# Selective scan of a four-layer network: VectorE's product goes to PSUM in one buffer, most decays go to SBUF and run three tiles ahead

## The chip, the cores and the metric

The kernel runs on one core of a Trainium2 chip as one program. The metric is device time in microseconds (us) from the first to the last instruction, the median of three runs. The core has five instruction queues that run side by side and meet through semaphores: TensorE (PE, with its weight loads shown as PEld), VectorE (DVE), ScalarE (ACT), GpSimd (POOL) and SyncE (SP, whose queue SPq issues the transfers). Each queue is worked off in its order, so an instruction that waits holds up all that stands behind it.

## The reference: what is computed

Four layers follow one another on a batch of 8 images of 56 x 56 pixels and 128 channels. Layers 0, 2 and 3 are deformable convolutions with their norms and feed-forward parts. Layer 1 is a visual state-space block, and the change is in it alone. It normalises and projects the image to 256 channels, convolves it, and then runs four scans over the pixels (rows and columns, forward and backward), each with 16 states for a channel:

```python
xs = jnp.stack([x0, x1, x0[..., ::-1], x1[..., ::-1]], axis=1)
...
dt = jax.nn.softplus(dt + dt_projs_b[None, :, :, None])
A = -jnp.exp(A_logs).reshape(K, Di, N)

def step(h, t):
    dt_t, u_t, B_t, C_t = t
    h = h * jnp.exp(dt_t[..., None] * A) + (dt_t * u_t)[..., None] * B_t[:, :, None, :]
    y = jnp.einsum('bkdn,bkn->bkd', h, C_t)
    return (h, y)
```

`exp(dt*A)` is called the decay here, `(dt*u)*B` the input of the scan. The four results are summed, normalised, gated, projected and put through a feed-forward part.

## The kernel before

The layers run one after the other: `tile_net` builds a `Dcn` for layers 0, 2 and 3 and a `Vss` for layer 1. The change is in `Vss.scans`, in its pools in `Vss.run`, and in one argument of the program's constructor.

**Tiling.** A step is one image, one of four directions `k`, and one of four chunks `c` of 784 pixels: 8 x 4 x 4 = 128 steps. Within a step there are 32 tiles of 128 partitions x 784 elements in fp32. A tile holds 32 channels x 4 states: `cg` counts 8 groups of channels, `sg` 4 groups of states, and `order` runs `sg` fastest. That makes 4096 tiles, listed in `units`. Four tiles with one `cg` are called a group below: 1024 groups.

**What a tile needs.** `decay` (L1343) makes `dA = exp(dt*A)` on ScalarE. `inputs` (L1348) makes the input: for `sg` 0 to 2 it is `u` on VectorE, from `dtu` (in PSUM) and `b` (in SBUF); for `sg` 3 it is `up` on GpSimd, from SBUF alone. The scan (L1449) is one VectorE instruction, which takes the decay, the input and a start value `st`, and writes `h` into SBUF. ScalarE saves the last column in `st` (L1452). GpSimd multiplies `h` by `c` (L1454) into `hc`. `add_sums` (L1372) lets TensorE add the products of two tiles into `acc`; `open_sums` (L1364) begins such a sum and `close_sums` (L1380) copies it out through ScalarE. `spread` (L1335) makes `dtu` for a whole group: two matmuls against the identity copy `dt*x` into PSUM.

**Buffers.** PSUM has room for eight banks of 512 elements. `misc` and `acc` take one each, `dtu` one buffer of two banks, and `dA` two buffers of two banks. In SBUF `u` has two buffers, `up` one, `h` three, `hc` six, and `dt` three.

**Order.** The loop over `units` (L1405) writes the instructions down in this order for the tile `now`: due sums, a piece of the next step's preparation, fetches, the decay of tile `now + 1`, the input of tile `now + 1` if it is VectorE's, at `sg == 1` the `spread` for the next group, the input two tiles ahead if it is GpSimd's, and then the scan of tile `now`. At its end `advance` adds a piece of background work: the first stage of the next image, or the last stage of this one, whose statistics run on VectorE and whose matmuls share the bank `misc`. A scheduler then moves instructions within that order. In the built program a group without background work stands on VectorE as u0 u1 s0 s1 u2 s2 s3, where s is a scan and the digit is `sg`.

`add_sums` is tied behind the last `spread` on TensorE by `issue_after`.

Of the kernel before, what the change touches and what calls it, by code (L numbers as in the profile page):

```python
# [41 lines left out]
F32 = mybir.dt.float32  # L42
BF16 = mybir.dt.bfloat16
I32 = mybir.dt.int32
AF = mybir.ActivationFunctionType
ALU = mybir.AluOpType
AX = mybir.AxisListType
PSUM = bass.MemoryType.PSUM
# [70 lines left out]
SC, SR = 784, 14  # L119
# [14 lines left out]
NCG, NSG = DI // TC, NST // TS  # L134
# [342 lines left out]
class Dcn:  # L477
# [9 lines left out]
    def run(self):  # L487
        tc, nc = self.tc, self.nc
        with ExitStack() as ctx:
            enter = ctx.enter_context  # L490
            self.cp = enter(tc.tile_pool(name="c_const", bufs=1))
            self.img = enter(tc.tile_pool(name="c_img", bufs=1))
            self.fp = enter(tc.tile_pool(name="c_front", bufs=1))
            self.up = enter(tc.tile_pool(name="c_unit", bufs=1))
            self.bp = enter(tc.tile_pool(name="c_block", bufs=3))
            self.tp = enter(tc.tile_pool(name="c_tail", bufs=1))
            self.pt = enter(tc.tile_pool(name="c_pt", bufs=3, space=PSUM))
            self.py = enter(tc.tile_pool(name="c_py", bufs=2, space=PSUM))
            self.pm = enter(tc.tile_pool(name="c_pm", bufs=3, space=PSUM))
            self.w = self.net.dcn_weights(self.layer, self.const)  # L500
            self.constants()
            self.split_bias()
            self.loop()
            self.check()
        over = nc.values_load(self.net.flag[:1, :1], min_val=0, max_val=1, skip_runtime_bounds_check_because="a comparison's result")
        with tc.If(over > 0):
            self.net.dcn_slow(self.layer, self.images, self.src, self.dst)
# [479 lines left out]
        nc.vector.tensor_scalar(net.flag, most, 0.0, None, ALU.is_gt)  # L987


class Vss:  # L990


# [6 lines left out]
    def run(self):  # L999
        tc = self.tc  # L1000
        with ExitStack() as ctx:
            enter = ctx.enter_context
            self.cp = enter(tc.tile_pool(name="v_const", bufs=1))
            self.img = enter(tc.tile_pool(name="v_img", bufs=1))
            self.prep = enter(tc.tile_pool(name="v_prep", bufs=1))
            self.work = enter(tc.tile_pool(name="v_work", bufs=2))
            self.bg = enter(tc.tile_pool(name="v_bg", bufs=1))
            self.dram = enter(tc.tile_pool(name="v_dram", bufs=2, space=DRAM))
            self.pmisc = enter(tc.tile_pool(name="v_misc", bufs=1, space=PSUM))
            self.pdtu = enter(tc.tile_pool(name="v_pdtu", bufs=1, space=PSUM))  # L1010
            self.pda = enter(tc.tile_pool(name="v_pda", bufs=2, space=PSUM))
            self.pacc = enter(tc.tile_pool(name="v_pacc", bufs=1, space=PSUM))
            self.weights()
            self.scans()
# [285 lines left out]
    def scans(self):  # L1300
        nc, w = self.nc, self.w
# [6 lines left out]
        units = [(at, t) for at in range(len(steps)) for t in range(NT)]  # L1308
# [13 lines left out]
        def advance(count):  # L1322
            for _ in range(count):
                while tasks:
                    try:
                        next(tasks[0])
                        break
                    except StopIteration:
                        tasks.popleft()

        def on_pool(t):

            return order[t][1] == NSG - 1

        def spread(at, t):  # L1335

            s, (cg, sg) = state[at], order[t]
            ps = s["dtu", cg] = self.pdtu.tile([128, 2, 512], F32, name="dtu", tag="dtu")
            for b in range(2):
                last = nc.tensor.matmul(ps[:, b, :SH], lhsT=self.net.ident, rhs=s["dt", cg][:, 1, SH * b : SH * (b + 1)], start=True, stop=True)  # L1340
            self.last_spread = last.ins

        def decay(at, t):  # L1343
            (i, k, c), s, (cg, sg) = steps[at], state[at], order[t]
            da = s["dA", t] = self.pda.tile([128, 1024], F32, name="dA", tag="dA")
            nc.scalar.activation(da[:, :SC], s["dt", cg][:, 0], AF.Exp, scale=w["A"][:, k, NSG * cg + sg : NSG * cg + sg + 1])  # L1346

        def inputs(at, t):  # L1348
            s, (cg, sg) = state[at], order[t]
            if on_pool(t):  # L1350
                u = self.work.tile([128, SC], F32, name="up", tag="up", bufs=1)
                nc.gpsimd.tensor_mul(u, s["dt", cg][:, 1], s["b", sg])  # L1352
            else:
                u = self.work.tile([128, SC], F32, name="u", tag="u", bufs=2)
                halves = [v.rearrange("p (x e) -> p x e", x=2) for v in (u, s["b", sg])]
                nc.vector.tensor_mul(halves[0], s["dtu", cg][:, :, :SH], halves[1])  # L1356
            s["u", t] = u
# [39 lines left out]
                    tasks.extend(self.output_stage(i, e) for e in (2 * c + 1, 2 * c))  # L1397

        spread(*units[0])
        decay(*units[0])  # L1400
        inputs(*units[0])
        st = ready = None
        group, late = [], deque()
        zeros = self.zeros()
        for now, (at, t) in enumerate(units):  # L1405
            (i, k, c), s, (cg, sg) = steps[at], state[at], order[t]
            forward = k < 2
            if t == 0:
                if at % NSC == 0:
                    st = self.prep.tile([128, NT], F32, name="st", tag="st", bufs=2)  # L1410
                    nc.gpsimd.memset(st, 0.0)
                if at % (NDIR * NSC) == 0 and i + 1 < self.images:
                    tasks.append(self.input_stage(i + 1))
                ready = iter(())
                if at + 1 < len(steps):
                    if steps[at + 1][0] > i:
                        self.load_xb(i + 1)
                    ready = self.prepare(state[at + 1], *steps[at + 1][1:])
            if t % (2 * NSG) == 0:
                late.append((now + 5, open_sums, (at, t)))  # L1420
            while late and late[0][0] <= now:
                _, do, args = late.popleft()
                do(*args)
            if t % 2 == 0:
                next(ready, None)

            if sg == 1:
                to = divmod(NCG * at + cg + 2, NCG)
                if to[0] < len(steps):
                    self.fetch_dt(state[to[0]], to[1])  # L1430
            if t in (3, 19):
                next(zeros, None)

            for x, when in enumerate(((25, 28, 29, 30), (26, 29, 30, 31))):
                if t in when and at + 1 < len(steps):
                    self.fetch_row(state[at + 1], x, when.index(t))
            if now + 1 < len(units):
                decay(*units[now + 1])
                if not on_pool(units[now + 1][1]):
                    inputs(*units[now + 1])  # L1440

                if sg == NSG - 3 and now + 3 < len(units):
                    spread(*units[now + 3])
            if now + 2 < len(units) and on_pool(units[now + 2][1]):
                inputs(*units[now + 2])
            hh = self.work.tile([128, SC], F32, name="h", tag="h", bufs=3)
            step = 1 if forward else -1
            u, dA = s.pop(("u", t)), s.pop(("dA", t))
            nc.vector.tensor_tensor_scan(hh[:, ::step], dA[:, :SC][:, ::step], u[:, ::step], st[:, t : t + 1], ALU.mult, ALU.add)  # L1449
            if c != (NSC - 1 if forward else 0):  # L1450
                last = SC - 1 if forward else 0
                nc.scalar.copy(st[:, t : t + 1], hh[:, last : last + 1])  # L1452
            hc = self.work.tile([128, SC], F32, name="hc", tag="hc", bufs=6)
            nc.gpsimd.tensor_mul(hc, hh, s["c", sg])  # L1454
            group.append((order[t], hc))
            if t % 2:
                late.append((now + 3, add_sums, (at, group)))
                group = []
                if t % (2 * NSG) == 2 * NSG - 1:
                    late.append((now + 5, close_sums, (at, t)))  # L1460
            if t % 2 or t % 4 == 0 or (i == self.images - 1 and k == 2):
                advance(1)
# [81 lines left out]
```

## Time and profile before

| what | value |
|---|---|
| time, median of 3 runs | 18469.42 us (18464.81 to 18477.36) |
| span of the profiled execution | 18479.8 us |
| layer 0, up to the first scans | 0 to 2366 us |
| scans of layer 1 | 2366 to 13801 us: 11435 us |
| layers 2 and 3 | 13801 to 18480 us: 4679 us |
| VectorE busy in the scans | 10264.5 us of 11435 |
| GpSimd busy in the scans | 10454.6 us of 11435 |
| ScalarE busy in the scans | 7051.7 us of 11435 |
| TensorE busy in the scans | 8638.3 us of 11435 |
| one VectorE scan, from `u` | 1838 ns, 3072 times |
| one VectorE `u` | 957 ns, 3072 times |
| one GpSimd `hc`, one `up` | 1873 ns, 4096 times; 1856 ns, 1024 times |
| one ScalarE decay | 915 ns, 4096 times |

The profiled execution is 10.4 us longer than the median of the runs. A duration in the profile reaches to the acknowledged end of an instruction; the next instruction of the same engine can start before that, so the distance from start to start can be shorter than the duration. Idle time of an engine is listed with what ended it (its releaser). In a row of the timeline, "x2" means that two equal instructions were merged.

### The profile page before, as it was taken

The page shows a single profiled execution, that of the slowest core. Times are in us where ns is not written, and L with a number is a line of the kernel's source. Part 1 is how long each engine was busy: PE and PEld are TensorE (multiplying, and loading weights), DVE is VectorE, ACT ScalarE, POOL GpSimd, SP SyncE. Part 2 cuts the span into 40 slices and gives each one's busy share as a digit, 9 for nine tenths or more (in the row PEclk, how much of TensorE's full clock was granted, in tenths as well). Part 3 has the DMA queues.
Part 4 walks back from the last instruction along what each step waited for, and adds up shares of the span by engine and source line. Part 5 has one row for each costly group of instructions (what it writes and reads, how often), then busy time and mean ns, then how long its engine had stood idle before and what let it go on. Part 6 is the DMA issues. An engine that isn't in the chain of part 4 may idle for free. (4 is left out here: it accounts for less than half of the span.)

```text
span 18479.8 us, 257190 instructions
## 1 busy us (share of the span) xinstructions
PE 13780.6 (75%) x89795; PEld 6844.2 (37%) x89795; DVE 15510.8 (84%) x18797; ACT 11145.4 (60%) x20690; POOL 11801.5 (64%) x6462
## 2 busy tenths in 40 slices
PE   5777787678678778678778768767665888577777
PEld 4555422222222222222222222222224666455555
DVE  8888379988988988988988898898985887688886
ACT  4666565566566566566566656656554666456666
POOL 2221089998998998998998998899981111222221
PEclk7878888889889889889888888888886888677777
DMA  7777444444443444344343443443433777577777
GB/s 215 205 210 200 122 158 160 162 158 148 142 149 137 146 147 140 140 150 139 140 150 136 143 152 135 143 150 136 147 122 110 196 198 198 143 204 204 201 204 175
DMA packets 1341779, 2961.90 MB, mean 160 GB/s; under 512 B 91168, under 2 KB 892132, under 8 KB 1325836
## 3 DMA queue, kind: packets, MB, share of 16 engines
q1 hardware_dynamic: 1340460, 2945.21, 51.4%
q8 instruction: 718, 11.76, 0.3%
q14 instruction: 601, 4.92, 0.1%
HBM read 2243.88 MB, written 866.92 MB: 168 GB/s over the span
## 5 line engine op out<-in xcount | busy, mean ns | idle before, releaser
L1454 POOL TENSOR_TENSOR hc<-h,c 128x784 f32<-128x784 f32 x4096 | 7560.9, 1873 | 764.2 <-DVE h L1449 534.4
L1449 DVE TENSOR_TENSOR_SCAN h<-dA,st,u 128x784 f32<-128x784 f32 x3072 | 5569.9, 1838 | 316.2 <-ACT dA L1346 182.3
L1346 ACT ACTIVATE dA<-dt,v_A 128x784 f32<-128x784 f32 x4096 | 3742.8, 915 | 719.1 <-DVE h L1449 717.8
L1356 DVE TENSOR_TENSOR u<-dtu,b 128x784 f32<-128x784 f32 x3072 | 2875.7, 957 | 559.9 <-PE dtu L1340 555.5
L1378 PE MATMUL acc<-hc,v_sum 128*32 128x392 f32 x16384 | 3222.3, 552 | 105.8 <-POOL hc L1454 105.6
L1340 PE MATMUL dtu<-dt,ident 128*128 128x392 f32 x4096 | 2105.1, 642 | 1512.1 <-issue 1102.6
L736 POOL TENSOR_TENSOR ay<-hat,om 112x756 f32<-112x756 f32 (+2 forms) x192 | 525.8, 2738 | 2750.0 <-ACT hat L727 2346.6
L1449 DVE TENSOR_TENSOR_SCAN h<-dA,st,up 128x784 f32<-128x784 f32 x1024 | 1876.7, 1833 | 242.4 <-POOL hc L1454 176.7
L1352 POOL TENSOR_TENSOR up<-dt,b 128x784 f32<-128x784 f32 x1024 | 1900.3, 1856 | 132.1 <-DVE h L1449 110.8
L807 ACT COPY st<-pt 128x448 f32<-128x448 f32 (+1 forms) x2240 | 1177.8, 542 | 1216.4 <-PE pt L805 1210.1
L1452 ACT COPY st<-h 128x1 f32<-128x1 f32 x3072 | 581.7, 189 | 2159.0 <-DVE h L1449 2150.5
L1340 PEld LDWEIGHTS dtu<-dt,ident 128*128 128x128 f32 x4096 | 862.0, 235 | 2564.6 <-issue 1672.2
L775 DVE TENSOR_TENSOR win<-win,patch 112x252 f32 (+2 forms) x3456 | 1695.4, 503 | 124.4 <-DVE win L775 34.2
L805 PE MATMUL pt<-ident,sw 112*128 112x112 f32 (+2 forms) x8960 | 1609.7, 310 | 199.1 <-DMA sw<-skew 198.8
L1378 PEld LDWEIGHTS acc<-hc,v_sum 128*32 128x32 f32 x16384 | 769.8, 117 | 2488.2 <-issue 1675.4
L766 POOL MEMSET win<- 128x1820 f32 (+2 forms) x384 | 630.1, 1646 | 1466.2 <-DMA skew<-win 1159.6
L821 PE MATMUL yps<-st,xw 128*32 128x48 f32 (+5 forms) x35840 | 1077.7, 245 | 397.6 <-ACT st L807 394.8
L805 PEld LDWEIGHTS pt<-ident,sw 112*128 112x128 f32 (+2 forms) x8960 | 1119.5, 161 | 485.6 <-DMA sw<-skew 166.9
L772 DVE TENSOR_TENSOR patch<-ay,hat 112x756 f32<-112x756 f32 (+2 forms) x1152 | 1221.3, 1066 | 22.5 <-POOL ay L736 19.5
L821 PEld LDWEIGHTS yps<-st,xw 128*32 128x32 f32 (+2 forms) x35840 | 757.0, 126 | 825.9 <-ACT st L807 476.1
L1112 PE MATMUL misc<-xn,v_tap 128*128 128x448 f32 x2016 | 867.3, 574 | 96.5 <-ACT xn L1146 61.2
L725 ACT ACTIVATE hat<-om,taps 112x252 f32<-112x252 f32 x1280 | 755.7, 729 | 287.1 <-DVE patch L772 273.4
(165 smaller groups left out, 19517.2 us busy)
## 6 DMA issues: line engine op xcount, KB each, us to landing
dt<-dds SPq DMA_DIRECT2D x1024, 784.0 KB
b<-rows SPq DMA_DIRECT2D x512, 392.0 KB
c<-rows SPq DMA_DIRECT2D x512, 392.0 KB
dds<-dd SPq DMA_DIRECT2D x256, 784.0 KB
sw<-skew SPq DMA_DIRECT2D x224, 812.0 KB
sw<-skew SPq DMA_DIRECT2D x224, 672.0 KB
sw<-skew SPq DMA_DIRECT2D x224, 588.0 KB
xw<-table SPq DMA_DIRECT2D x224, 320.0 KB
```

The lines of the kernel that those rows point to most:

```text
L772: nc.vector.tensor_mul(patch[:n], bcast(a, 3, KX), bcast(b, 2, KY))
L775: self.last_add = nc.vector.tensor_add(to, to, patch[:n, NCB * p : NCB * (p + 1)]).ins
L805: last = nc.tensor.transpose(ps[:m, n * g : n * (g + 1)], sw[:n, g, p : p + m], self.net.ident[:n, :n])
L807: nc.scalar.copy(st[:m], ps[:m, : G * n])
L821: self.nc.tensor.matmul(yps[CG * g : CG * (g + 1), t0:t1], lhsT=xw[:m, k + part, CG * g : CG * (g + 1)], rhs=st[:m, at + t0 : at + t1], st ...
L1340: last = nc.tensor.matmul(ps[:, b, :SH], lhsT=self.net.ident, rhs=s["dt", cg][:, 1, SH * b : SH * (b + 1)], start=True, stop=True)
L1346: nc.scalar.activation(da[:, :SC], s["dt", cg][:, 0], AF.Exp, scale=w["A"][:, k, NSG * cg + sg : NSG * cg + sg + 1])
L1352: nc.gpsimd.tensor_mul(u, s["dt", cg][:, 1], s["b", sg])
L1356: nc.vector.tensor_mul(halves[0], s["dtu", cg][:, :, :SH], halves[1])
L1378: nc.tensor.matmul(acc[r : r + TC, :SH], lhsT=w["sum"], rhs=hc[:, SH * b : SH * (b + 1)], start=False, stop=sg == NSG - 1)
L1449: nc.vector.tensor_tensor_scan(hh[:, ::step], dA[:, :SC][:, ::step], u[:, ::step], st[:, t : t + 1], ALU.mult, ALU.add)
L1454: nc.gpsimd.tensor_mul(hc, hh, s["c", sg])
```

## The change

Five edits, all but the last in `Vss`:

- VectorE's `u` is put into PSUM, in a pool `v_pu` of one buffer of two banks; before, it was in SBUF with two buffers.
- The decays of the tiles with `sg` 0 to 2 go to SBUF, with four buffers. The decay of `sg` 3 stays in PSUM under the name `dAp`, and its pool has one buffer in place of two. PSUM is as full as before: 1 + 1 + 2 + 2 + 2 banks.
- Decays are written down three tiles ahead (`AHEAD`), before it was one.
- VectorE's input is written down with its own tile, just ahead of the scan that reads it; before, it was one tile ahead. `spread` for the next group follows at `sg == 2` and no longer at `sg == 1`. GpSimd's input stays two tiles ahead.
- The scratch space for descriptors of DMAs made by software is set to 8192 bytes a partition, half of the default.

```diff
+AHEAD = 3
...
-            self.pda = enter(tc.tile_pool(name="v_pda", bufs=2, space=PSUM))
+            self.pda = enter(tc.tile_pool(name="v_pda", bufs=1, space=PSUM))
+            self.pu = enter(tc.tile_pool(name="v_pu", bufs=1, space=PSUM))
...
-            da = s["dA", t] = self.pda.tile([128, 1024], F32, name="dA", tag="dA")
-            nc.scalar.activation(da[:, :SC], s["dt", cg][:, 0], AF.Exp, scale=w["A"][:, k, NSG * cg + sg : NSG * cg + sg + 1])
+            if on_pool(t):
+                da = s["dA", t] = self.pda.tile([128, 1024], F32, name="dAp", tag="dAp")[:, :SC]
+            else:
+                da = s["dA", t] = self.work.tile([128, SC], F32, name="dA", tag="dA", bufs=4)
+            nc.scalar.activation(da, s["dt", cg][:, 0], AF.Exp, scale=w["A"][:, k, NSG * cg + sg : NSG * cg + sg + 1])
...
-                u = self.work.tile([128, SC], F32, name="u", tag="u", bufs=2)
+                u = self.pu.tile([128, 1024], F32, name="u", tag="u")[:, :SC]
...
-        decay(*units[0])
-        inputs(*units[0])
+        for x in range(AHEAD):
+            decay(*units[x])
...
-            if now + 1 < len(units):
-                decay(*units[now + 1])
-                if not on_pool(units[now + 1][1]):
-                    inputs(*units[now + 1])
-
-                if sg == NSG - 3 and now + 3 < len(units):
-                    spread(*units[now + 3])
+            if now + AHEAD < len(units):
+                decay(*units[now + AHEAD])
+            if not on_pool(t):
+                inputs(at, t)
+            if sg == NSG - 2 and now + 2 < len(units):
+                spread(*units[now + 2])
...
-            nc.vector.tensor_tensor_scan(hh[:, ::step], dA[:, :SC][:, ::step], u[:, ::step], st[:, t : t + 1], ALU.mult, ALU.add)
+            nc.vector.tensor_tensor_scan(hh[:, ::step], dA[:, ::step], u[:, ::step], st[:, t : t + 1], ALU.mult, ALU.add)
...
-    nc = bacc.Bacc("TRN2", target_bir_lowering=False, num_devices=1)
+    nc = bacc.Bacc("TRN2", target_bir_lowering=False, num_devices=1, dynamic_dma_scratch_size=8192)
```

In the built program a group without background work now stands on VectorE as u0 s0 u1 s1 u2 s2 s3.

## The prediction

> **What bounds the kernel now.** I read the windows by stage first, then what VectorE waited for inside the scans, then VectorE's timeline, instruction by instruction. The windows give us, then the busy time of each engine with its instruction count:
>
> ```profile
> core 0: us, PE busy (x) PEld busy (x) DVE busy (x) ACT busy (x) POOL busy (x), PEclk, DMA share, GB/s
> ...
> 2366.00:13801.00 11435.00, 8638.25 (x31302) 3030.31 (x31302) 10264.50 (x8600) 7051.73 (x13027) 10454.60 (x5762) 0.86 0.41 145
> ```
>
> VectorE is busy for 90% of the scans and GpSimd for 91%: two engines near full that feed each other. ScalarE, at 62%, is not a limit by its sum. What VectorE waited for in that window (us in total, times, longest):
>
> ```profile
> DVE u L1356 <- PE dtu L1340: 473.5, 258, 7.8
> DVE h L1449 <- ACT dA L1346: 234.3, 199, 4.2
> DVE h L1449 <- POOL hc L1454: 214.4, 165, 3.2
> ```
>
> So late decays cost VectorE 234 us, a full set of `h` buffers 214 us, and a late `dtu` 474 us. VectorE's timeline (start, us, instruction) shows what it pays to wait for itself:
>
> ```profile
> 2504.72 0.95 DVE L1356 TENSOR_TENSOR u<-dtu,b 128x784 f32<-128x784 f32 x1
> 2505.58 1.84 DVE L1449 TENSOR_TENSOR_SCAN h<-dA,st,up 128x784 f32<-128x784 f32 x1
> 2507.34 0.95 DVE L1356 TENSOR_TENSOR u<-dtu,b 128x784 f32<-128x784 f32 x1
> 2508.21 1.84 DVE L1449 TENSOR_TENSOR_SCAN h<-dA,st,u 128x784 f32<-128x784 f32 x1
> 2510.08 0.97 DVE L1356 TENSOR_TENSOR u<-dtu,b 128x784 f32<-128x784 f32 x1
> ...
> 8009.96 0.95 DVE L1356 TENSOR_TENSOR u<-dtu,b 128x784 f32<-128x784 f32 x1
> 8011.04 1.85 DVE L1449 TENSOR_TENSOR_SCAN h<-dA,st,u 128x784 f32<-128x784 f32 x1
> 8012.81 1.82 DVE L1449 TENSOR_TENSOR_SCAN h<-dA,st,up 128x784 f32<-128x784 f32 x1
> ```
>
> The scan at 2508.21 reads the `u` of 2504.72. It starts 0.87 us after the `u` in front of it, before that one's 0.95 us are over: neighbours that don't depend on each other overlap. The `u` at 2510.08 goes into the buffer that the scan just before it read (every second `u` has the same one): it starts 1.87 us after that scan, where 2505.58 to 2507.34 took 1.76. The scan at 8011.04 reads the `u` directly before it: 1.08 us from start to start. I took these distances over all starts in the window:
>
> - `u` then a scan that doesn't read it: median 0.881 us (1250 pairs); a scan that reads it: 1.083 us (610 pairs). A wait for a write just made costs 0.202 us.
> - scan then a `u` into another buffer: 1.742 us; into the buffer just read: 1.874 us (108 pairs). That wait costs 0.132 us.
>
> A clean group before is thus 0.865 + 0.882 + 1.757 + 1.742 + 1.083 + 1.767 + 1.742 = 9.84 us. Of the 1023 distances from one group's last scan to the next's, 315 lie between 9.5 and 10 us and the 25th percentile is 9.84: in a third of its groups VectorE's own instructions set the pace. The mean is 11.17.
>
> **The change part by part.**
>
> *One buffer for u, written just ahead of its scan.* In the built order every scan of `u` waits for VectorE itself, and every second and third `u` of a group waits for the scan before it. Neighbours of the first kind rise from 610 to 2509 (elsewhere a statistic of the background work stands between and fills the wait), of the second kind from 108 to 1703:
> 1899 x 0.202 = +384 us, 1595 x 0.132 = +211 us, together +595 us. A clean group becomes 3 x 1.083 + 2 x 1.874 + 1.767 + 1.742 = 10.51 us, +0.67. All of it lies on VectorE, behind which stand the scan, then GpSimd's `hc` and ScalarE's `st`. What could hide it is a wait at the same scan for another engine; those are the 234 and 214 us, which I count as removed below, not twice.
>
> The Trainium skill speaks against this price, on VectorE: DVE Perf Modes, section "The DRAIN you can't avoid": chained copies cost the same with a semaphore after each as with one at the end. By that rule these 595 us would be nothing and the sum would be a gain of 325 us. This trace disagrees, 1.083 against 0.881 us, and I go by the trace.
>
> *u in PSUM instead of SBUF.* No VectorE row before writes PSUM, so the acknowledgement that the scan waits for has no price. From below: ScalarE's decay (to PSUM) overlaps its successor by some 0.062 us where its copies to SBUF overlap by 0.101, so a write to PSUM may end 0.04 us sooner: 2509 x -0.04 = -100 us. From above: the tail of `u` (0.951 less 0.865) doubled, 2509 x 0.086 = +216 us. I take 0, as `u` already reads PSUM and keeps its form.
>
> Another rule of the skill would add to it: Perfetto Trace Analysis, section "Optimizing Scalar/DVE Operations", puts VectorE's fixed access at about 60 ns for SBUF and 125 ns for PSUM. By it the 3072 writes would cost some 200 us more (an estimate from that page); no row here shows it.
>
> *The scan reads dA from SBUF and u from PSUM.* One operand in each, as before. The two kinds of scan differ by 5 ns in the mean (1838 and 1833): 0, within 3072 x 0.015 = 46 us either way by their medians (1841 and 1826).
>
> *Decays three tiles ahead, in five buffers.* Three more of them may be in flight than VectorE needs next, some 8 us of cover, while ScalarE's longest background piece (two table loads of 1.28 us around an operation of 1.51) is 4.1 us. I take nine tenths of the 234 us away: -210 us; bounds 0 and -234. A decay into SBUF costs ScalarE no more: its SBUF operation L1268 of the same size has 855 ns against 915. Decays are moved past `st` copies (L1452), which wait for scans; they no longer wait themselves for a scan one tile back (718 us of ScalarE's idle time). They issue no transfer. The transfer of `dt` waits for the last decay on the old buffer (4123 us of SPq's waits): that one and the next use both come two tiles earlier. 0.
>
> *GpSimd.* Its starts are 1.805 us apart at best: 5120 x 1.805 + 508 of the preparation's (968 us) + 106 for L1189 + 31 for memsets = 10,350 us, against 10,380 for VectorE (1024 x 9.84, less 414 x 0.202 for the broken pairs, + 386 of other instructions). After the change VectorE needs 10,975 and GpSimd has over 600 us to spare, so VectorE should wait for it less. I take half of the 218 us (`hc` and `up`): -110; bounds 0 and -218.
>
> *spread one tile later in the order.* It still becomes free when the third `u` has been read and is still wanted two scans later: the window from u2's end to the next u0 is 1.083 + 1.767 + 1.742 - 0.951 = 3.64 us, before 3.44 to 3.64; the two matmuls take 1.6. In the trace the late ones stand behind background matmuls (L1112's three taps take 3.4 us), whose number is unchanged. 0 for the 474 us; bounds -200 (ScalarE frees `misc` sooner) and +200 (the spread now stands behind sums written a tile earlier).
>
> *Half the scratch space.* All transfers in the page's list are issued by SPq, and its queues are "hardware_dynamic" and "instruction": no software descriptors. 0; if that is wrong, layers 0, 2 and 3 (7045 us) change.
>
> Sum: 18,479.8 + 595 - 210 - 110 = 18,755 for the span. The median of the runs is 10 below the span: **18,745 us**. With the bounds of the single terms, not all at one end: 18,600 to 18,980.
>
> **The rivals.**
>
> *Faster: ScalarE freed frees TensorE too.* ScalarE stands 718 us behind scans for a decay's buffer, with background copies queued behind it, and TensorE's `misc` matmuls stand behind those, the spread behind them. Then decays and `dtu` both come in time. VectorE's waits for others are about 1170 - 81 (its own, 610 x 0.133 of gap) = 1090 us; if four tenths remain, 654 us go, against 595: 18,410. It decides once more than 633 us of waits are gone (595 and the bound of 0.2%). Against: the `st` copies still wait for scans (2150 us) and hold up the same ScalarE queue.
>
> *No change: GpSimd is the bound.* It is busy 91%, and VectorE's added waits would come out of its own idle 1170 us: 18,470. Against: a third of the groups run at VectorE's sum, and VectorE waited for GpSimd for only 218 us.
>
> *Slower still: TensorE's spread is late.* In the built order `open_sums` stands directly ahead of the spread in 214 of 1024 groups, before in none; it waits for ScalarE's copy of the old sum (L1370, 570 us in 297 waits, 1.9 us each). The spread's slack is 3.6 - 1.6 = 2.0 us; if waits of that length begin only when the spread could, 214 x 1.9 = +400, of which I take three quarters: 19,045. It decides where those waits end more than 2 us after u2. Against: before, open and four sums stood ahead of the spread too, and late ones were behind other matmuls.
>
> **How the numbers follow.** My forecast 0.60, faster 0.15, no change 0.11, slower still 0.14. A measurement here can tell about 0.2% from none (37 us). From the forecast's lower bounds a little falls to "same". Faster 0.15, same 0.10, slower 0.75. The range reaches to the no-change case and the edge of the fast one, and to the slow one: 18,420 to 19,060.
>
> **What would show it.** Right: VectorE's timeline with u, scan, u, scan about 1.08 and 1.87 us apart; the commonest group near 10.5 us; VectorE's waits for `dA` under 30 us; the scans' window near 11,710 us; the layers outside unchanged. Wrong: 0.88 from `u` to its scan (PSUM writes acknowledge sooner), or a window that grows by less than 100 us with fewer waits for `dtu` (the freed ScalarE), or waits for `dtu` well over 474 us (TensorE), or layers 0, 2, 3 that move (the scratch space).

## The result and the profile after

The changed kernel is slower: 18881.43 us (median of 4 runs, 18874.88 to 18885.9) against 18467.11 us for the kernel before, run beside it (4 runs, 18463.75 to 18477.36). The ratio is 1.0223, with a 95% interval of 1.0208 to 1.0237: +414 us. The forecast was 18,745 us in a range of 18,420 to 19,060, so the sign was right, the range held, and the time was 136 us too low.

All of it is in the scans. The profiled execution has a span of 18873.3 us. From the first scan to the last `hc` it takes 11,837 us, before 11,437 (+400); the rest takes 7036 us, before 7043. The windows view of after over the scans (us, then busy time of each engine with its instruction count):

```profile
core 0: us, PE busy (x) PEld busy (x) DVE busy (x) ACT busy (x) POOL busy (x), PEclk, DMA share, GB/s
2354.00:14192.00 11838.00, 9229.15 (x31312) 3123.32 (x31314) 10618.34 (x8606) 7122.23 (x13037) 10487.05 (x5764) 0.87 0.39 140
```

VectorE's busy time rose by 354 us, though its instructions are nearly as many (8606 against 8600) and of the same kinds. Their durations add up to only 60 us more; the other 293 us are overlap of neighbours, which fell from 601 to 308 us. GpSimd does the same work in a longer window, so it is further from its limit than before. The granted clock is the same within 0.01.

VectorE's timeline of after, in a group without background work (start, us, instruction, in brackets the idle time before it and what ended that):

```profile
8062.68 0.98 DVE L1363 TENSOR_TENSOR u<-dtu,b 128x784 f32<-128x784 f32 x1 [0.94 <-PE dtu L1344]
8063.79 1.85 DVE L1455 TENSOR_TENSOR_SCAN h<-dA,st,u 128x784 f32<-128x784 f32 x1
8065.67 0.98 DVE L1363 TENSOR_TENSOR u<-dtu,b 128x784 f32<-128x784 f32 x1
8066.79 1.85 DVE L1455 TENSOR_TENSOR_SCAN h<-dA,st,u 128x784 f32<-128x784 f32 x1
8068.67 0.98 DVE L1363 TENSOR_TENSOR u<-dtu,b 128x784 f32<-128x784 f32 x1
8069.78 1.85 DVE L1455 TENSOR_TENSOR_SCAN h<-dA,st,u 128x784 f32<-128x784 f32 x1
8071.55 1.82 DVE L1455 TENSOR_TENSOR_SCAN h<-dAp,st,up 128x784 f32<-128x784 f32 x1
```

From start to start it is 1.11 us from `u` to its scan and 1.88 from the scan to the next `u`, again and again: each of these instructions waits for the one before it. Over the window 2509 scans stand directly behind their own `u` (median 1.115 us), and 1703 times a `u` stands directly behind the scan that frees its buffer (1.881). The commonest group takes 10.5 to 11 us (599 of 1023, 25th percentile 10.59); before, it was 9.5 to 10 us in 315 of them.

What VectorE waited for in the scans of after (us in total, times, longest):

```profile
DVE u L1363 <- PE dtu L1344: 489.2, 243, 10.1
DVE bn_st L1073 <- PE misc L1177: 130.1, 68, 4.4
DVE xt L1202 <- PE misc L1199: 82.5, 38, 6.7
DVE h L1455 <- POOL hc L1460: 45.4, 75, 1.8
DVE xt L1231 <- PE misc L1228: 36.1, 12, 6.7
...
DVE h L1455 <- ACT dA L1353: 1.5, 3, 0.5
```

Against before: late decays 234 to 1.5 us, late GpSimd 218 to 52 (`hc` and `up`), late `dtu` 474 to 489. New in size are the waits for `misc`: the background statistics (`bn_st`) and copies (`xt`) wait 249 us for TensorE, before 96:

```profile
DVE bn_st L1069 <- PE misc L1173: 45.4, 29, 2.6
...
DVE xt L1198 <- PE misc L1195: 30.7, 22, 3.9
DVE xt L1227 <- PE misc L1224: 19.9, 24, 1.7
```

And TensorE's wait for `hc`, at the sums of the scans' products, before and after:

```profile
PEld acc L1378 <- POOL hc L1454: 648.9, 758, 2.7
```

```profile
PEld acc L1385 <- POOL hc L1460: 1796.7, 1537, 5.8
```

Nearly three times as much. The prediction had no term for that row.

### The profile page after: what moved, and what is told of

It is laid out like the page before. It is cut to its first block, busy times and chain, and to the rows that moved or that the text cites. A ratio compares the mean times of both kernels' runs of the same rounds, so it can differ in the third digit from the quotient of the medians.

```text
span 18873.3 us, 258033 instructions
## 1 busy us (share of the span) xinstructions
PE 14354.5 (76%) x89795; PEld 6933.3 (37%) x89795; DVE 15874.8 (84%) x18797; ACT 11212.7 (59%) x20697; POOL 11797.3 (63%) x6462
## 5 line engine op out<-in xcount | busy, mean ns | idle before, releaser
L1455 DVE TENSOR_TENSOR_SCAN h<-dA,st,u 128x784 f32<-128x784 f32 x3072 | 5666.5, 1845 | 347.1 <-POOL hc L1460 8.5
L1385 PE MATMUL acc<-hc,v_sum 128*32 128x392 f32 x16384 | 3638.1, 548 | 764.6 <-POOL hc L1460 754.7
L1363 DVE TENSOR_TENSOR u<-dtu,b 128x784 f32<-128x784 f32 x3072 | 2992.6, 974 | 629.7 <-PE dtu L1344 570.0
L1353 ACT ACTIVATE dA<-dt,v_A 128x784 f32<-128x784 f32 x3072 | 2892.6, 945 | 501.9 <-DVE h L1455 498.7
L1344 PE MATMUL dtu<-dt,ident 128*128 128x392 f32 x4096 | 2195.3, 668 | 956.2 <-issue 633.6
L1385 PEld LDWEIGHTS acc<-hc,v_sum 128*32 128x32 f32 x16384 | 836.5, 117 | 3517.8 <-POOL hc L1460 1796.7
L1455 DVE TENSOR_TENSOR_SCAN h<-dAp,st,up 128x784 f32<-128x784 f32 x1024 | 1869.7, 1826 | 44.5 <-POOL hc L1460 36.9
L1353 ACT ACTIVATE dAp<-dt,v_A 128x784 f32<-128x784 f32 x1024 | 936.8, 915 | 147.0 <-DVE h L1455 145.7
```

Source lines behind the costliest of these rows:

```text
L1353: nc.scalar.activation(da, s["dt", cg][:, 0], AF.Exp, scale=w["A"][:, k, NSG * cg + sg : NSG * cg + sg + 1])
L1385: nc.tensor.matmul(acc[r : r + TC, :SH], lhsT=w["sum"], rhs=hc[:, SH * b : SH * (b + 1)], start=False, stop=sg == NSG - 1)
L1455: nc.vector.tensor_tensor_scan(hh[:, ::step], dA[:, ::step], u[:, ::step], st[:, t : t + 1], ALU.mult, ALU.add)
```

## The experiments

Each kernel was timed beside the kernel before on the same chip; differences are to that run's own before (18459.9 to 18481.4 us). The kernels e2, e5 to e10 and e12 have the halved scratch space of the change too, which e4 prices by itself.

### The parts one by one

**e1_u_in_sbuf**: the changed kernel with `u` back in SBUF, still in one buffer, and its PSUM pool left out.

```diff
-                u = self.pu.tile([128, 1024], F32, name="u", tag="u")[:, :SC]
+                u = self.work.tile([128, SC], F32, name="u", tag="u", bufs=1)
...
-    nc = bacc.Bacc("TRN2", target_bir_lowering=False, num_devices=1, dynamic_dma_scratch_size=8192)
+    nc = bacc.Bacc("TRN2", target_bir_lowering=False, num_devices=1, dynamic_dma_scratch_size=4096)
```

> The changed kernel with u back in SBUF, still one buffer and still just ahead of its scan (the scratch space goes to 4096 bytes to make room). Theory (VectorE waits for itself): the change stays almost whole; only the longer write into PSUM goes, from u to its scan 1.110 us back to 1.083 in some 2540 pairs, -70 us, and the other wait 1.881 to 1.874, -12: about 18,800 us. Rival (the write to PSUM itself is the loss): back to 18,470 to 18,550 us.

Measured: 22,283.96 us, ratio 1.2054 [1.2034, 1.2074], +3806; neither expectation held. The costliest groups of its page (xcount, busy us, mean ns of one, then idle time):

```profile
L1459 POOL TENSOR_TENSOR hc<-h,c 128x784 f32<-128x784 f32 x4096 | 9500.9, 2343 | 1484.2 <-DVE h L1454 1361.4 <-PE acc L1384 52.9 <-DVE bn_mv L1073 16.1
L1454 DVE TENSOR_TENSOR_SCAN h<-dA,st,u 128x784 f32<-128x784 f32 x3072 | 8128.7, 2646 | 586.2 <-POOL hc L1459 267.6 <-ACT dA L1352 2.4 <-DVE u L1362 2.4
L1454 DVE TENSOR_TENSOR_SCAN h<-dAp,st,up 128x784 f32<-128x784 f32 x1024 | 1877.2, 1833 | 926.5 <-POOL hc L1459 899.2 <-ACT dd L1269 6.9 <-ACT sp L1272 5.1
```

Scans with the decay in PSUM keep their 1833 ns; those with both inputs in SBUF take 2646 in the mean, and GpSimd's `hc` 2343 in place of 1873. So with the decays in SBUF, the move of `u` to PSUM is what spares the scans this price. The kernel says nothing of the price of a write to PSUM, for which it was made; e3 does.

**e2_decays_ahead_alone**: the kernel before with two decays in four in SBUF and all of them three tiles ahead; `u` as before.

```diff
-            da = s["dA", t] = self.pda.tile([128, 1024], F32, name="dA", tag="dA")
+            if sg % 2:
+                da = s["dA", t] = self.pda.tile([128, 1024], F32, name="dAp", tag="dAp")[:, :SC]
+            else:
+                da = s["dA", t] = self.work.tile([128, SC], F32, name="dA", tag="dA", bufs=2)
...
-        decay(*units[0])
+        for x in range(3):
+            decay(*units[x])
...
+            if now + 3 < len(units):
+                decay(*units[now + 3])
...
-                decay(*units[now + 1])
```

> The kernel before with its two u buffers in SBUF and u one tile ahead, but decays three tiles ahead in four buffers (sg 1 and 3 in PSUM, sg 0 and 2 in SBUF). Theory (the decays ahead are a gain that VectorE's self-waits outweighed): the 234 us of waits for decays go, waits for h buffers stay near 214, pairs of u and its own scan rise from 610 to 754 (+29 us): about 18,270 us, range 18,150 to 18,350. Rival (the decays ahead bring nothing, since GpSimd is as full as VectorE): 18,440 to 18,490 us.

Measured: 20,805.34 us, ratio 1.1254 [1.1235, 1.1272], +2327. Neither expectation held. Its groups show why, side by side in one kernel:

```profile
L1459 POOL TENSOR_TENSOR hc<-h,c 128x784 f32<-128x784 f32 x4096 | 8792.9, 2173 | 1000.1 <-DVE h L1454 808.9 <-PE acc L1381 116.2 <-PE dtu L1340 14.1
L1454 DVE TENSOR_TENSOR_SCAN h<-dA,st,u 128x784 f32<-128x784 f32 x2048 | 6056.2, 2957 | 169.4 <-POOL hc L1459 67.9 <-ACT st L1457 1.5 <-DVE u L1359 1.5
L1454 DVE TENSOR_TENSOR_SCAN h<-dAp,st,u 128x784 f32<-128x784 f32 x1024 | 1864.3, 1821 | 98.0 <-POOL hc L1459 98.0
```

The second and third row are the same instruction with a `u` in SBUF; what differs is the home of the decay, and the one takes 2957 ns, the other 1821.

**e3_u_order_alone**: the kernel before with one `u` buffer (in SBUF), `u` written with its own tile, and the spread one tile later; decays as before.

```diff
-                u = self.work.tile([128, SC], F32, name="u", tag="u", bufs=2)
+                u = self.work.tile([128, SC], F32, name="u", tag="u", bufs=1)
...
-        inputs(*units[0])
...
-                if not on_pool(units[now + 1][1]):
-                    inputs(*units[now + 1])
-
-                if sg == NSG - 3 and now + 3 < len(units):
-                    spread(*units[now + 3])
+            if not on_pool(t):
+                inputs(at, t)
+            if sg == NSG - 2 and now + 2 < len(units):
+                spread(*units[now + 2])
```

> The kernel before with one edit: one u buffer (in SBUF), u written just ahead of its scan, and spread one tile later with it; decays as before. Theory (VectorE waits for itself): 2467 pairs of u and its scan at 1.083 us and 1741 of scan and next u at 1.874 us, +590 us, less some 150 us of waits for GpSimd, and the waits for decays stay near 234 us or fall a little as VectorE is slower: 18,850 to 18,950 us. Rival (the loss comes from PSUM or from the decays in SBUF): under 18,600 us. The moved spread alone: if the waits of the statistics for the misc bank rise here too (96 us before, 249 us in the changed kernel), they come from this edit.

Measured: 18,959.18 us, ratio 1.026 [1.0243, 1.0278], +481: one buffer and this order by themselves cost more than the whole change. From `u` to its scan it takes 1.108 us here, where `u` is in SBUF, against 1.115 in the changed kernel: the write to PSUM adds 7 ns, some 18 us over 2509 pairs. TensorE's wait for `hc` is 1879 us, and the statistics' waits 239, both near the changed kernel's. VectorE's two longest waits:

```profile
DVE u L1356 <- PE dtu L1340: 424.1, 256, 82.1
DVE h L1447 <- ACT dA L1346: 250.4, 220, 4.3
```

The 82.1 us are one wait before the first scan; without it `dtu` is waited for 342 us.

**e4_scratch_alone**: the kernel before with the scratch space halved.

```diff
-    nc = bacc.Bacc("TRN2", target_bir_lowering=False, num_devices=1)
+    nc = bacc.Bacc("TRN2", target_bir_lowering=False, num_devices=1, dynamic_dma_scratch_size=8192)
```

> The kernel before with half the scratch space for descriptors and nothing else. All theories but one: no change, 18,450 to 18,490 us. Rival (the scratch space carries transfers of this kernel): longer, above all in layers 0, 2 and 3.

Measured: 18,482.28 us, ratio 1.0002 [0.9992, 1.0012]. No cost is seen.

**e9_lead_of_one**: the changed kernel with `AHEAD = 1`.

```diff
-AHEAD = 3
+AHEAD = 1
```

> The changed kernel with decays one tile ahead in place of three; all buffers and places as changed. It prices the lead alone. Theory (the lead takes VectorE's waits for decays away, and that was worth what those waits were before): they come back, 160 to 250 us as in the kernels with decays one ahead, and the time is 18,960 to 19,100 us. Rival (the four SBUF buffers did it, or the waits for decays lie beside others): 18,870 to 18,920 us.

Measured: 18,894.6 us, ratio 1.022 [1.0203, 1.0237], +413, as much as the change. VectorE's wait for decays:

```profile
DVE h L1455 <- ACT dA L1353: 6.5, 9, 0.9
```

So the lead written in the code is worth nothing that these runs can tell; the five buffers take the wait away, and the scheduler uses them by itself. When a scan begins, 3.1 decays beyond its own are finished on average in this kernel, 3.2 in the changed kernel and 0.3 in the kernel before.

### The order and the buffer apart

**e11_order_alone_two_buffers**: e3 with a single number changed.

```diff
-                u = self.work.tile([128, SC], F32, name="u", tag="u", bufs=1)
+                u = self.work.tile([128, SC], F32, name="u", tag="u", bufs=2)
```

> The kernel with u's written order alone (18,959 us) with one number changed: two u buffers in SBUF and not one. Theory (the single buffer is what holds VectorE): pairs of u and its own scan fall from 2467 to 532 and pairs of scan and the next u on its buffer from 1741 to 9 or fewer; the time falls by 250 to 350 us to 18,610 to 18,710. What is then left above the kernel before is the price of the later written spread, 130 to 230 us. Rival (the written order is what costs): 18,850 us or more.

Measured: 18,613.52 us, ratio 1.0078 [1.0061, 1.0094], +154. So one buffer in place of two costs 481 - 154 = 328 us, and the order of writing 154 us on its own. In the built program `u` stands directly ahead of its scan only 532 times here (before 610): with a second buffer the scheduler moves it ahead by itself. The 154 us are therefore not from waits for a `u` just written. They show elsewhere: TensorE's wait for `hc` is 2309 us (before 649), and VectorE's wait for decays 455 (before 234):

```profile
PEld acc L1378 <- POOL hc L1452: 2308.8, 1836, 5.8
...
DVE h L1447 <- ACT dA L1346: 455.4, 327, 4.8
```

**e7_sums_behind_spread**: the changed kernel with the sums that are due written just behind the spread, where they stood ahead of it.

```diff
-            while late and late[0][0] <= now:
-                _, do, args = late.popleft()
-                do(*args)
...
             if sg == NSG - 2 and now + 2 < len(units):
                 spread(*units[now + 2])
+            while late and late[0][0] <= now:
+                _, do, args = late.popleft()
+                do(*args)
```

> The changed kernel with the due sums written behind the spread and no longer ahead of it. Rival to VectorE's self-waits (TensorE stands behind GpSimd's products with the spread and the background's matmuls queued behind): TensorE's waits of sums for GpSimd fall from 1795 to near 650 us and VectorE's waits for statistics from 249 to near 96, about 18,730 us or less. Theory (VectorE's self-waits): no more than that 150 us can go, and the clean group stays at 10.6 us; if TensorE only waits since VectorE is slower, 18,860 to 18,900.

Measured: 18,779.45 us, ratio 1.0167 [1.015, 1.0184], +303: 112 us less than the change, between the two expectations. TensorE's wait for `hc` falls from 1796.7 us to

```profile
PEld acc L1385 <- POOL hc L1460: 463.1, 612, 3.0
```

while the commonest group stays (628 groups from 10.5 to 11 us): that part belongs to the one buffer. VectorE's waits for the statistics fall from 249 to 218 us, where the rival expected 96; those for `dtu` fall from 489 to 440, for transfers from 27 to 6.

**e5_two_u_buffers**: `u` of `sg` 0 and 2 in PSUM, of `sg` 1 in SBUF, one buffer each, written one tile ahead with the spread as before; the decays that meet a PSUM `u` in SBUF (three buffers), the others in PSUM (one).

```diff
-            da = s["dA", t] = self.pda.tile([128, 1024], F32, name="dA", tag="dA")
+            if sg % 2:
+                da = s["dA", t] = self.pda.tile([128, 1024], F32, name="dAp", tag="dAp")[:, :SC]
+            else:
+                da = s["dA", t] = self.work.tile([128, SC], F32, name="dA", tag="dA", bufs=3)
...
-                u = self.work.tile([128, SC], F32, name="u", tag="u", bufs=2)
+                if sg == 1:
+                    u = self.work.tile([128, SC], F32, name="us", tag="us", bufs=1)
+                else:
+                    u = self.pu.tile([128, 1024], F32, name="u", tag="u")[:, :SC]
...
+            for x, odd in ((1, 1), (3, 0)):
+                if now + x < len(units) and order[units[now + x][1]][1] % 2 == odd:
+                    decay(*units[now + x])
...
-                decay(*units[now + 1])
```

> The decays ahead without the single u buffer, and with one SBUF input for each scan as before: u of sg 0 and 2 in PSUM, of sg 1 in SBUF, written one tile ahead, spread where it was before; decays of sg 0 and 2 in SBUF three tiles ahead, of sg 1 and 3 in one PSUM buffer one tile ahead. Theory (one u buffer makes VectorE wait for itself; decays ahead are a gain): 671 pairs of u and its scan as against 610 before, hardly any late decay, scans all near 1.84 us: 18,260 us, range 18,200 to 18,350. Rival (decays ahead bring nothing, as GpSimd is full too): 18,440 to 18,490. If scans with the decay in SBUF again take over 2 us although u is in PSUM, two SBUF inputs are not the reason of the long scans in the two kernels above.

Measured: 18,417.23 us, ratio 0.9968 [0.9956, 0.9981], -60: a small gain, short of the range of the theory. All kinds of scan take 1828 to 1838 ns: `u` in PSUM and the decay in SBUF is as good as the reverse. VectorE waits 146 us for decays in the one PSUM buffer (1 us for those in SBUF) and 242 for GpSimd.

**e6_second_buffer_only**: the homes of e5 with the change's order (`u` with its own tile, the spread at `sg == 2`).

```diff
-        inputs(*units[0])
...
-            if now + 1 < len(units):
-                if not on_pool(units[now + 1][1]):
-                    inputs(*units[now + 1])
-
-                if sg == NSG - 3 and now + 3 < len(units):
-                    spread(*units[now + 3])
+            if not on_pool(t):
+                inputs(at, t)
+            if sg == NSG - 2 and now + 2 < len(units):
+                spread(*units[now + 2])
```

> The same places as in the run above, but u written with its own tile and spread one tile later, as in the changed kernel: against that one the second u buffer is what differs (and the home of the decay of sg 1). Theory: with a second buffer the scheduler puts u ahead by itself (549 pairs of u and its scan, hardly a u behind its reader), so the self-waits go: 18,260 to 18,400 us, clean groups at 9.8 us and not 10.6. What it is above the run above is the price of the moved spread; if the statistics' waits for the misc bank come from the moved spread they stay near 250 us here and the time is some 150 us above. Rival (the decays in SBUF or their lead cost the 412 us): near 18,880.

Measured: 18,604.86 us, ratio 1.0071 [1.0054, 1.0088], +128. Again `u` is moved ahead without being told (549 directly ahead of their scans), and a cost remains, 188 us over e5. It is not the statistics' waits for `misc`, which are 122 us here and not near 250.

**e12_two_buffers_sums_behind**: e6 with the due sums written behind the spread, the same edit as in e7.

```diff
-            while late and late[0][0] <= now:
-                _, do, args = late.popleft()
-                do(*args)
...
             if sg == NSG - 2 and now + 2 < len(units):
                 spread(*units[now + 2])
+            while late and late[0][0] <= now:
+                _, do, args = late.popleft()
+                do(*args)
```

> The kernel with the second u buffer (18,605 us) with the due sums written behind the spread. If the later spread costs its 188 us since sums stand ahead of it on TensorE, waiting for GpSimd, all of it goes: 18,400 to 18,450 us. If only the 102 us that the same edit gave the changed kernel: about 18,500 us. If something else of the later spread costs: 18,580 to 18,620 us.

Measured: 18,370.12 us, ratio 0.9953 [0.9937, 0.997], -90, and 218 us under e6; more than was expected, as moving the sums took back all that the later spread cost. The waits of e6 and e12 in the scans show the way from the sums to VectorE, first TensorE's, then ScalarE's at the copy of a finished sum, then VectorE's. e6:

```profile
PEld acc L1385 <- POOL hc L1461: 2390.0, 1812, 5.8
...
ACT y L1396 <- PE acc L1385: 710.5, 261, 6.8
...
ACT out L1396 <- PE acc L1385: 316.8, 114, 6.4
...
DVE h L1456 <- ACT dAp L1350: 280.5, 206, 4.4
```

e12:

```profile
PEld acc L1385 <- POOL hc L1461: 699.6, 843, 3.8
...
ACT y L1396 <- PE acc L1385: 327.0, 197, 4.1
...
ACT out L1396 <- PE acc L1385: 122.1, 68, 6.4
...
DVE h L1456 <- ACT dAp L1350: 72.0, 83, 3.6
```

With the sums ahead, TensorE stands for GpSimd's newest `hc`; ScalarE stands at its copies of the sums (1027 us against 449), and the decays queued behind those copies come late (281 us against 72). These 209 us are about the difference of the two scan windows, 11,544 and 11,333 us; VectorE's other waits nearly cancel (for `st` 53 us less, for TensorE 18 less, for GpSimd 59 more, for transfers 18 more). In the changed kernel, whose decays have five buffers, they no longer come late, and there the same edit is worth 112 us and not 218.

### A longer lead for u

**e8_u_two_ahead**: the kernel before with `u` two tiles ahead in three SBUF buffers, and the spread at `sg` 0.

```diff
-                u = self.work.tile([128, SC], F32, name="u", tag="u", bufs=2)
+                u = self.work.tile([128, SC], F32, name="u", tag="u", bufs=3)
...
+        inputs(*units[1])
...
-                if not on_pool(units[now + 1][1]):
-                    inputs(*units[now + 1])
-
-                if sg == NSG - 3 and now + 3 < len(units):
-                    spread(*units[now + 3])
+            if now + 2 < len(units) and not on_pool(units[now + 2][1]):
+                inputs(*units[now + 2])
+            if sg == NSG - 4 and now + 4 < len(units):
+                spread(*units[now + 4])
```

> The kernel before with u two tiles ahead in three SBUF buffers, spread at sg 0, decays as before in PSUM. No u directly ahead of its scan (610 x 0.20 = -123 us), and four scans in place of two between the last u of a group and the first of the next, so the waits for dtu fall from 474 to under 150 us: 18,030 us, range 17,950 to 18,250. Rival (GpSimd, busy 91%, takes the gain back as waits for h buffers): 18,300 to 18,400.

Measured: 18,374.34 us, ratio 0.9943 [0.9926, 0.996], -102; the theory had said 18,030, the rival 18,300 to 18,400. VectorE's waits:

```profile
DVE h L1449 <- ACT dA L1346: 377.7, 187, 5.2
DVE h L1449 <- POOL hc L1454: 287.3, 238, 7.4
DVE u L1356 <- PE dtu L1340: 284.3, 242, 5.4
```

The wait for `dtu` fell by 190 us, and the waits for decays and for `hc` rose by 143 and 73: most of the gain turned into new waits.

**e10_u_and_decays_two_ahead**: e8 with the decays two tiles ahead as well.

```diff
+        decay(*units[1])
...
-            if now + 1 < len(units):
-                decay(*units[now + 1])
+            if now + 2 < len(units):
+                decay(*units[now + 2])
```

> u two tiles ahead in three SBUF buffers as in the fastest kernel so far (18,374 us), with decays written two tiles ahead in their two PSUM buffers. Theory (a decay can't start before the scan two tiles back frees its buffer, whatever the lead): its 378 us of waits for decays fall by less than half, 18,200 to 18,380 us. Rival (ScalarE held up in order behind a decay that waits for a scan): 18,400 to 18,600 us.

Measured: 18,361.29 us, ratio 0.9932 [0.9915, 0.9948], -120. The waits for decays fall to 215 us and those for `hc` rise to 365. e8, e10 and e12 agree within what these runs can tell; all three beat the kernel before by 0.5 to 0.7%, and the changed kernel by more.

## Why the prediction was right in sign and low in size

| part | forecast, us | what the runs give, us |
|---|---|---|
| one buffer for `u`, with fewer waits for GpSimd | 595 - 110 = +485 | +328 (e3 less e11) |
| order of writing, spread one tile later | 0 | +154 (e11) |
| decays in five buffers, `u` in PSUM | -210 | -67 (the change less e3) |
| scratch space (its measured part is within the row above) | 0 | +4, interval over zero (e4) |
| sum, without the scratch space | +275 | +415 by the rounded parts; the change measured +414 |

The last column is a chain of kernels that differ by one part each; another order of the parts could share them out differently. The other route shows the same two costs in other sizes: e12 -90, sums ahead of the spread +218 (e6), one buffer and the home and buffers of one decay +286 (the change).

That the forecast came within 136 us owes something to luck: by the chain, one buffer was put 157 us too high, and the order and the decays 154 and 143 us too low. The first took away half of the other two.

VectorE's own time in the scans can be added up a second way, by what it waited for (us):

| VectorE in the scans | before | after | difference | forecast |
|---|---|---|---|---|
| waits for itself: lost overlap 293, gaps 313, longer durations 60 | | | +666 | +595 |
| waits for ScalarE | 247 | 5 | -242 | -210 |
| waits for GpSimd | 218 | 52 | -166 | -110 |
| waits for TensorE (`dtu` and the statistics) | 570 | 738 | +168 | 0 |
| other waits | 53 | 27 | -26 | 0 |
| window of the scans | 11,437 | 11,837 | +400 | +275 |

The first row is what the other rows leave of the window. By this account the term that was missed is TensorE's: 16 us at `dtu` and 153 at the statistics. The two accounts differ as the parts hide one another's waits: the cost of the later spread stands in e11 in the row of ScalarE, and the five buffers empty that row.

**One buffer: right, and the larger part.** VectorE's timeline has the pattern and the counts that were forecast (2509 and 1703 pairs). The price of a pair was a little low: 1.115 us against 1.083. A `u` that itself begins after a wait lasts longer, in PSUM (982 ns against 956) and in SBUF (975 against 947). By the medians the own waits measure 2509 x 0.234 - 610 x 0.202 = 464 and 1703 x 0.139 - 108 x 0.132 = 222, together 686 us, near the 666 of the table and above the 595 forecast. The net price from e11 to e3 is half of that, since a later scan takes other waits away: VectorE's waits for itself rise by 664 us, while those for ScalarE fall from 495 to 280 and those for GpSimd from 162 to 47. The prediction named this hiding, but counted those waits in its terms for the decays and GpSimd instead. The two kinds of wait were not tested apart.

The Trainium skill, VectorE: DVE Perf Modes, section "The DRAIN you can't avoid", found no extra cost in a semaphore between chained copies. Between e11 and e3 only the number of buffers differs, and it is worth 328 us; for these instructions the measurement decides against the rule. (A gain without the 595 us would have been 320 us, not the 325 that the prediction gives: 210 + 110.)

**u in PSUM: near 0, as forecast.** The pair `u` and scan takes 1.108 us with `u` in SBUF (e3) and 1.115 in PSUM (the change), 7 ns more. It is not the same in every program: in e5, 671 such pairs with `u` in PSUM have a median of 1.061 us, under the 1.083 of the kernel before; why was not settled. The Trainium skill, Perfetto Trace Analysis, section "Optimizing Scalar/DVE Operations", puts VectorE's access at about 60 ns for SBUF and 125 ns for PSUM. No such difference of 65 ns shows in these pairs.

**Decays: the waits went as said, the time did not.** 234 us fell to 1.5, and yet decays in SBUF with `u` in PSUM brought 67 us. The step that failed is taking a wait's whole length as time won. Against e3, VectorE's waits for ScalarE fell by 274 us, but its waits for `dtu` rose from 342 to 489: with the decays in time, more than half of what was won is waited at `dtu` instead. The lead of three, to which the prediction gave the gain, has no part in it (e9).

**spread one tile later: a cost that was put at 0.** The prediction took it for free, with a rival in which sums opened ahead of the spread made `dtu` late. The rival had the right queue and the wrong victim: waits for `dtu` went from 474 to 489 us only. The sums are due at a fixed tile, and the spread moved past that point in the order; `add_sums` is tied behind the last spread written. With the spread first, the sums more often found `hc` ready; with the sums first, TensorE waits for the `hc` just being made (649 to 1797 us). Who then pays depends on the rest: in e11 and e6 ScalarE's copies and the decays behind them. In the changed kernel, which has decays in store, it is no single row: e7's gain is spread over `dtu`, the statistics and the transfers. e7 and e12 take the sums back behind the spread and win 112 and 218 us.

**Statistics: partly open.** Their waits are 239 us in e3 and still 218 in e7, both with one buffer, and 74 to 122 in e11 and e6 with two. One buffer therefore has more part in them than the sums; by what way was not settled.

**The rivals.** GpSimd as the bound falls: it waited more for VectorE after the change (1046 us for `h`, before 534), and VectorE's waits for itself lengthened the window. TensorE freed by ScalarE falls: waits for `dtu` did not shrink. The scratch space falls (e4).

## What to carry to other kernels

On an engine that sets the pace, the instruction before should not make what the next one reads, nor free what it writes: a second buffer was worth 328 us here, and with it the scheduler found the lead by itself. When a step is moved within a written order, list what now stands ahead of it on every queue it uses, and ask whether that waits for something newer than before; who pays is found in the waits of the other engines too. A wait removed need not be a gain of its length: here 274 us of waits for ScalarE went, 147 us came back at `dtu`, and 67 us were won. Look which wait stands beside it.

## What was not expected of the hardware

A scan whose two inputs are both in SBUF collides with GpSimd's multiplications. In e2 it took 2957 ns against 1821 with the decay in PSUM, in e1 single ones up to 11 us, and GpSimd's `hc` went from 1873 to 2173 and 2343 ns; the kernels became 12.5% and 20.5% slower. That GpSimd is the cause shows in e1's trace: 31 of these scans had no GpSimd multiplication beside them and took 1848 ns in the mean, 2230 had one beside them for at least nine tenths of their time and took 2360. The Trainium skill states the rule in SBUF — State Buffer, section "Who interferes with whom": a VectorE instruction with two SBUF inputs contends with a GpSimd instruction that reads SBUF. These runs agree with it. So in these kernels one input of each scan should be in PSUM; which one does not matter (e5).

ScalarE's decay takes 945 ns into SBUF and 915 into PSUM; the prediction had put this at no difference. ScalarE, busy for 7122 of 11,838 us after the change, has room for it.
